# Fixing every engine's order by the source in a four-layer graph network, with row work spread in small steps

## The chip, the cores and the metric

The kernel runs on one core of a Trainium2 chip. The metric is the device time of one execution in microseconds (us). The core has a matrix engine (PE, TensorE), a vector engine (DVE), an activation engine (ACT, ScalarE), a general engine (POOL, GpSimd) and SP, whose queue issues the large transfers here. Each takes its instructions in the order of its own queue; semaphores let one wait for another.

## The reference

`x` has 4096 rows of 64 numbers, `adj` is a 4096 x 4096 matrix of zeros and ones. Four layers follow one another, each as `x = layernorm(x + layer(x, adj))`:

```python
# layer 0
deg = clip(sum(adj, axis=1) + 1, 1)
h = (adj @ x + x) / deg
z = relu(concat([x, h]) @ W + b)
out = z / max(norm(z), 1e-12)
# layers 1 and 3 (hyperbolic attention; logmap between every pair of rows)
x_t = logmap0(x)
adj_att = sigmoid(left[:, None] + right[None, :] + b_att) * adj    # left, right = x_t @ w_att halves
out = proj(expmap(x, einsum('ij,ijd->id', adj_att, logmap(x[:, None], x[None, :]))))
# layer 2
mask = adj != 0; rank = cumsum(mask, axis=1); deg = rank[:, -1:]
k = minimum(deg, 100); pos = rank - (deg - k)
out = (mask * where(pos > 0, 0.5 ** (k - pos), 0)) @ (x @ weight) + bias
```

## The kernel before

The rows are in 4 groups of 1024 (`GROUPS`, taken from 3 down to 0), the neighbours in 32 blocks of 128 (`BLOCKS`, from 31 down). Every layer reads the whole of `adj` again, as 64 loads of 1 MB (`load`, tile `edges`, five buffers, issued by SP at L614); one load holds two blocks for one group.

*Layer 0.* For each load PE multiplies both blocks with split values of x (L1087, four matmuls a block). `check` (L692) lets DVE look at every second load whether all its entries are zeros and ones. After 16 loads of a group ACT copies the sums out (`top`, L1107), PE multiplies them with the weights, and DVE divides by the degree (L1118). Then `end_0`, `norm_rows` and `prepare` follow for the group: they are the *row work*, dozens of dependent DVE operations on 128x8 numbers, some on 128x512 values, with copies on ACT (`ys`, `yd`, `hi_lo` and so on), transposes on PE (L775) and small products.

*Layers 1 and 3* (`attention`, `attend`). A *unit* is one block against one group of 1024 rows. PE forms the pair products `zp` in PSUM with six matmuls (L861, L864, L867), ACT makes `sig` (sigmoid, L869) and `sq` (square of zp, L873), DVE makes `t = max(zp, 0) * sig` (L875) and `t = (sq + const) * t` (L876), and PE adds `xe.T @ t` to the sums `acc` with two f32 matmuls (L878, four in the profile's count). `zp`, `sig` and `sq` have two buffers, `t` three. After 32 units ACT copies the sums, and `move` does the group's row work: 80 or so small operations, a Square and a tanh on ACT, two products on POOL (L912, L988), the last addition at L992. In layer 1 `linear` follows: transposes (L1001), a copy (`x_t`, L1004), products (L1008), halves by ACT (L1016) and DVE (L1017). `spread_left` (L837, L842) makes the left column of the next group for ACT.

*Layer 2* has two passes of two groups each. For 64 units a pass, PE forms the ranks `z` (L1209), ACT the weights `w` (exp, L1217), PE the sums (L1220). `end_2`, `norm_rows` and `prepare` are the row work behind it.

*The order.* Row work is written as generators in a list `waiting`, first in first out. `tick(rate)` runs the next steps of the first one between two units: three per load in layer 0, two, then one per unit in layer 1, four, then one in layer 3, one in layer 2. That is the order in the source only: the framework's scheduler reorders the instructions of each engine's queue as it thinks best before the kernel is built, and the pools of layer 1, 2 and 3 open and close between stages. A step's operations may all depend on each other. At the end a fallback under `If(fit < P)` is there; it was not taken.

Of the kernel before, what the change touches and what calls it, by code (L numbers as in the profile page):

```python
# [10 lines left out]
F32 = mybir.dt.float32  # L11
F16 = mybir.dt.float16
# [7 lines left out]
P = 128  # L20
N = 4096
D = 64
# [36 lines left out]
def gnn_stack_kernel(  # L59
# [511 lines left out]
    def stream(fits):  # L571

        with ExitStack() as st:

# [5 lines left out]
            loads = pool("f_loads", 5)  # L580
# [8 lines left out]
            waiting = []  # L589

            def tick(n):
                while n and waiting:
                    if next(waiting[0][1], False) is False:
                        waiting.pop(0)
                    else:
                        n -= 1

            def later(tag, *steps):
                def all_steps():
                    for part in steps:  # L600
                        yield from (part or ())

                waiting.append((tag, all_steps()))

            def need(tag):
                while any(t == tag for t, _ in waiting):
                    tick(1)
# [10 lines left out]
            def grp(name, bufs=None):  # L618
                kw = {"bufs": bufs} if bufs else {}
                return row.tile([P, WB, D], F32, name=name, **kw)  # L620

            def nums(name, n=WB):
                return row.tile([P, n], F32, name=name)
# [4 lines left out]
            def rsqrt(a, name):  # L628

                n = a.shape[1]  # L630
                half = row.tile([P, n], I32, name="rs_half")
                V.tensor_scalar(half, a.bitcast(I32), 1, None, ALU.logical_shift_right)
                r, t = nums(name, n), nums("rs_t", n)
                V.tensor_scalar(
                    r.bitcast(I32), half, -1.0, float(0x5F3759DF), ALU.mult, ALU.add
                )
                for _ in range(3):
                    V.tensor_mul(t, r, r)
                    V.scalar_tensor_tensor(t, t, -0.5, a, ALU.mult, ALU.mult)
                    V.scalar_tensor_tensor(r, t, 1.5, r, ALU.add, ALU.mult)  # L640
                return r
# [20 lines left out]
            ys = keep.tile([P, WB, 3 * D + 10], F16, name="ys")  # L662
            yd = keep.tile([P, WB, D + 10], F16, name="yd")
            es, ed = ys[:, :, 3 * D :], yd[:, :, D:]
            rest = (ROOT - 2.0) * UNIT
            for k in range(3):
                part = float(np.float16(rest))
                nc.gpsimd.memset(es[:, :, k], part)
                rest -= part
            nc.gpsimd.memset(ed[:, :, 0:3], 1.0)  # L670
            nc.gpsimd.memset(es[:, :, 3:5], 1.0)
            nc.gpsimd.memset(ed[:, :, 5:7], 1.0)

            def att_columns(w_att, name):


                w = row.tile([P, 2], F32, name="att_w")
# [18 lines left out]
            def curved(c, name):  # L696

                c2, sc = num(keep, name + "_c2", 1), num(keep, name + "_sc", 1)
                rsc, of_y = num(keep, name + "_rsc", 1), num(keep, name + "_of_y", 1)
                V.tensor_scalar(c2, c, -2.0, None, ALU.mult)  # L700
                V.tensor_copy(rsc, rsqrt(c, "rsc"))
                V.tensor_mul(sc, rsc, c)
                V.tensor_scalar(of_y, rsc, -((2.0 * UNIT) ** -0.5), None, ALU.mult)
                V.tensor_scalar(sc, sc, -((2.0 * UNIT) ** 0.5), None, ALU.mult)
                return c, c2, sc, rsc, of_y

            def norm_rows(x, s, v, x2_to):

                m, v2, sq = nums("n_m"), nums("n_v2"), grp("sq")
                V.tensor_reduce(m, v, AX.X, ALU.add)  # L710
                V.tensor_scalar(m, m, 1.0 / D, None, ALU.mult)
                yield 1
                V.tensor_sub(v, v, over(m))
                nc.scalar.activation(sq, v, AF.Square)
                yield 1
                yield 1
                V.tensor_reduce(v2, sq, AX.X, ALU.add)
                yield 1
                V.tensor_scalar(m, v2, 1.0 / D, 1e-5, ALU.mult, ALU.add)
                r = rsqrt(m, "n_r")  # L720
                yield 1
                V.tensor_mul(x[:, blocks(s), :], v, over(r))
                V.tensor_mul(x2_to, r, r)
                V.tensor_mul(x2_to, x2_to, v2)
                yield 1

            def prepare(s, x, att, b_att, curve, least, good):

                c, c2, sc, rsc, of_y = curve
                at, cols = blocks(s), slice(s * WW, (s + 1) * WW)  # L730
                xg, bg, rbg = x[:, at, :], b[:, at], rb[:, at]
                V.tensor_scalar(cx2[:, at], x2[:, at], c, None, ALU.mult)
                V.tensor_scalar(bg, cx2[:, at], -1.0, 1.0, ALU.mult, ALU.add)
                V.reciprocal(rbg, bg)

                V.tensor_scalar(rbg, rbg, -0.13, 0.0, ALU.max, ALU.min)

                m, y = nums("m"), grp("z0")
                V.tensor_scalar(m, rbg, sc, None, ALU.mult)
                V.tensor_mul(y, xg, over(m))  # L740
                nc.scalar.copy(ys[:, :, :D], y)
                yield 1
                nc.scalar.copy(ys[:, :, 2 * D : 3 * D], y)
                nc.scalar.copy(yd[:, :, :D], y)
                hl = row.tile([P, WB, 2], F16, name="hl")
                V.tensor_scalar(hl[:, :, 0], rbg, UNIT, None, ALU.mult)
                V.scalar_tensor_tensor(hl[:, :, 1], rbg, UNIT, hl[:, :, 0], ALU.mult, ALU.subtract)
                nc.gpsimd.tensor_copy(es[:, :, 5:7], hl)
                nc.gpsimd.tensor_copy(es[:, :, 7:9], hl)
                nc.gpsimd.tensor_copy(es[:, :, 9], hl[:, :, 0])  # L750
                nc.gpsimd.tensor_copy(ed[:, :, 3:5], hl)
                for k, of in ((7, 0), (8, 0), (9, 1)):
                    nc.gpsimd.tensor_scalar(
                        ed[:, :, k], hl[:, :, of], -2.0 / UNIT, None, ALU.mult
                    )
                V.tensor_sub(ys[:, :, D : 2 * D], y, ys[:, :, :D])
                yield 1

                g, w = nums("g"), grp("w_att")
                V.tensor_scalar(g, cx2[:, at], 1.0, 1.0 / D, ALU.add, ALU.mult)  # L760
                V.tensor_scalar(m, rbg, CUBE / UNIT, None, ALU.mult)
                V.tensor_add(w, xg, over(g))
                yield 1
                V.tensor_mul(xe[:, at, :], w, over(m))
                yield 1
                for into, rows_of in (
                    (hi_lo, ys[:, :, : 2 * D]),
                    (lo_hi, ys[:, :, D : 3 * D]),
                    (src, ys[:, :, 2 * D :]),
                    (dst, yd),  # L770
                ):
                    n = rows_of.shape[2]
                    t = aux.tile([P, WW], F16, name="aux")
                    for k in range(WB):
                        nc.tensor.transpose(  # L775
                            t[:n, k * P : (k + 1) * P], rows_of[:, k, :], ident16
                        )
                    yield 1
                    nc.scalar.copy(into[:, cols], t[:n])
                    yield 1  # L780


                q, q1, rt, t = nums("q"), nums("q1"), nums("rt"), nums("tt")
                V.tensor_scalar(q, x2[:, at], least, c, ALU.max, ALU.mult)
                V.tensor_scalar(q1, q, SMALL, None, ALU.max)
                rt = rsqrt(q1, "rt")
                yield 1
                V.tensor_mul(t, q1, rt)
                V.tensor_scalar(t, t, TOP, None, ALU.min)
                V.tensor_scalar(q1, q1, QTOP, None, ALU.min)  # L790
                nc.scalar.activation(t, t, AF.Ln, bias=1.0)
                nc.scalar.activation(q1, q1, AF.Ln, bias=1.0, scale=-1.0)
                yield 1
                f = nums("f")
                V.tensor_scalar(q, q, SMALL, SHIFT, ALU.min, ALU.add)
                V.scalar_tensor_tensor(q, q, 0.2, q, ALU.mult, ALU.mult)
                yield 1
                V.scalar_tensor_tensor(f, q1, -0.5, t, ALU.mult, ALU.add)
                V.tensor_mul(f, f, rt)
                V.scalar_tensor_tensor(f, f, SERIES0, q, ALU.add, ALU.add)  # L800
                V.tensor_scalar(m, bg, of_y, None, ALU.mult)
# [528 lines left out]
```

## Time and profile before

| what | value |
|---|---|
| median of 3 runs | 1247.65 us (1246.52 to 1258.46) |
| the profiled execution | 1248.49 us, its span 1246.8 us |
| mean granted clock of PE | 0.95 |
| busy: PE, DVE, ACT, POOL | 85%, 79%, 65%, 4% of the span |
| L875 and L876, mean of one | 1219 and 1220 ns, 256 each |
| L869 and L873, mean of one | 1143 and 1114 ns, 256 each |
| L692 (`check`) | 2288 ns, 64 |
| loads of `edges` | 256 of 1 MB |

The stages, as the first big instruction of each shows them in the timeline:

| stage | from, us | to, us |
|---|---|---|
| layer 0 (first load issued to first L875) | 5.0 | 223.5 |
| layer 1, starts of the groups | 223.5, 311.9, 412.1, 513.0 | 597.4 (last L875) |
| layer 2 (L1217) | 619.5 | 854.8 |
| layer 3, starts of the groups | 860.7, 960.4, 1042.4, 1129.3 | 1215.0 (last L875) |
| last group's row work, store, fallback's test | 1215.0 | 1246.8 |

A line such as "PE aux L775 <- DVE ys L756: 25.8, 5, 7.6" means: PE's instructions of L775 waited 25.8 us in total for DVE's instruction of L756, 5 times, the longest 7.6 us. In a timeline each row has its start, its length, the engine, the line and the operation, and in brackets the idle time of the engine before it and what ended that. The digits of the busy rows are tenths of 40 equal slices.

### The profile page before, as it was taken

How to read it: one execution, taken by the hardware profiler on the slowest of the kernel's cores; microseconds unless marked ns; L12 is line 12 of the kernel's file. 1: busy time of each engine (PE TensorE's matmuls, PEld its weight loads, DVE VectorE, ACT ScalarE, POOL GpSimd, SP SyncE). 2: the span in 40 equal slices, each digit the busy share in tenths (PEclk: the TensorE clock that was granted, in tenths of full speed). 3: DMA queues.
4: the chain of work that ended last, by engine and by line, in shares of the span. 5: the costliest groups of instructions: out<-in, count | busy, mean ns of one | idle time of the engine just before them, and what ended most of it. 6: DMA issues, size and time to landing. Idle time of an engine off the chain costs nothing.

```text
span 1246.8 us, 13844 instructions
## 1 busy us (share of the span) xinstructions
PE 1064.1 (85%) x4818; PEld 393.4 (32%) x4907; DVE 981.3 (79%) x2081; ACT 811.4 (65%) x833; POOL 49.6 (4%) x85
## 2 busy tenths in 40 slices
PE   5879788899998899798598898898889999899990
PEld 2345445232222322322232223332333333222220
DVE  5486876999997799599663347535999999999996
ACT  0021213889886787587365668767889888788870
POOL 0010101000000000000100000000000000001001
PEclk9989899899999799699699999999999999999996
DMA  7989898555554366155177887688345555565510
GB/s 280 400 338 335 313 357 324 186 175 203 202 203 169 109 201 229 68 203 186 51 268 271 295 313 265 241 295 299 134 152 201 203 202 203 182 204 204 203 34 20
DMA packets 40144, 271.83 MB, mean 218 GB/s; under 512 B 6016, under 2 KB 6272, under 8 KB 7296
## 3 DMA queue, kind: packets, MB, share of 16 engines
q1 hardware_dynamic: 37440, 269.50, 61.0%
q10 hardware_dynamic: 2624, 1.35, 0.4%
q8 instruction: 40, 0.66, 0.2%
q14 instruction: 40, 0.33, 0.1%
HBM read 269.78 MB, written 1.05 MB: 217 GB/s over the span
## 4 chain that ended last, share of the span: by engine, by line
DVE 40%; PE 40%; ACT 12%; DMA 4%; issue 3%; POOL 1%; another core or an unknown queue 0%; ACTq 0%; POOLq 0%; SPq 0%; DVEq 0%
DVE t L875 14%; DVE t L876 13%; PE acc L878 7%; PE z L1209 6%; PE acc L1220 6%; ACT w L1217 5%; PE zp L861 4%; PE zp L864 4%; PE zp L867 4%; PE acc L1087 4%; ACT sq L873 3%; DVE junk L692 3%; DMA edges<-in_adj_dram 2%; PE aux L1008 2%; PE aux L775 1%
## 5 line engine op out<-in xcount | busy, mean ns | idle before, releaser
L873 ACT ACTIVATE sq<-zp,turn 128x1024 f32<-128x1024 f32 x256 | 285.1, 1114 | 84.1 <-PE zp L867 52.9
L875 DVE SCALAR_TENSOR_TENSOR t<-zp,sig 128x1024 f32<-128x1024 f32 x256 | 311.3, 1219 | 15.3 <-ACT sq L873 12.9
L876 DVE SCALAR_TENSOR_TENSOR t<-sq,t 128x1024 f32<-128x1024 f32 x256 | 311.0, 1220 | 0.8
L869 ACT ACTIVATE sig<-left_b,right 128x1024 f32<-128x1024 f32 x256 | 292.1, 1143 | 19.9 <-DVE t L875 18.0
L878 PE MATMUL acc<-t,xe 128*64 128x512 f32 x1024 | 282.2, 624 | 16.6 <-DVE t L876 15.9
L692 DVE SCALAR_TENSOR_TENSOR junk<-edges 128x2048 bf16<-128x2048 f32 x64 | 146.4, 2288 | 94.2 <-DMA edges<-in_adj_dram 94.2
L861 PE MATMUL zp<-edges,two_i 128*128 128x512 bf16 x461 | 181.3, 393 | 37.8 <-DVE t L875 34.1
L864 PE MATMUL zp<-lo_hi,hi_lo 128*128 128x512 f16 x512 | 195.5, 382 | 3.7 <-issue 0.4
L867 PE MATMUL zp<-dst,src 74*128 74x512 f16 x512 | 196.7, 384 | 0.0
L1217 ACT ACTIVATE w<-z,at_edge 128x1024 bf16<-128x1024 f32 x128 | 136.1, 1113 | 76.3 <-PE z L1209 74.0
L861 PEld LDWEIGHTS <-two_i 128*128 128x128 bf16 x512 | 50.2, 98 | 178.9 <-issue 141.7
L1220 PE MATMUL acc<-w,halves 128*64 128x512 bf16 x512 | 80.9, 393 | 25.0 <-ACT w L1217 24.5
L1087 PE MATMUL acc<-edges,first 128*128 128x512 bf16 x240 | 79.0, 406 | 16.7 <-DMA edges<-in_adj_dram 16.3
L878 PEld LDWEIGHTS acc<-t,xe 128*64 128x64 f32 x1024 | 51.8, 136 | 124.5 <-DVE t L876 64.6
L1209 PE MATMUL z<-edges,enter 128*128 128x512 bf16 x245 | 85.4, 393 | 2.2 <-DVE k L909 1.6
L1087 PE MATMUL acc<-edges,third 128*65 128x512 bf16 x256 | 83.2, 407 | 0.8 <-issue 0.2
L867 PEld LDWEIGHTS <-src 74*128 74x128 f16 x512 | 49.4, 96 | 101.0 <-issue 42.2
L864 PEld LDWEIGHTS <-hi_lo 128*128 128x128 f16 x512 | 50.1, 98 | 86.0 <-issue 50.3
L1209 PE MATMUL z<-edges,pass_by 128*128 128x512 bf16 x237 | 75.0, 394 | 1.7 <-issue 1.5
L1220 PEld LDWEIGHTS <-halves 128*64 128x64 f16 x512 | 24.1, 108 | 75.6 <-issue 74.6
L1107 ACT COPY top<-acc 128x512 f32<-128x512 f32 x8 | 4.7, 588 | 63.7 <-PE acc L1087 63.7
L1209 PEld LDWEIGHTS <-enter 128*128 128x128 bf16 x256 | 24.2, 97 | 52.3 <-issue 28.9
(255 smaller groups left out, 784.4 us busy)
## 6 DMA issues: line engine op xcount, KB each, us to landing
edges<-in_adj_dram SPq DMA_DIRECT2D x256, 1024.0 KB, 5.0
x<-in_x_dram SPq DMA_DIRECT2D x4, 256.0 KB, 3.9
out_dram<-x ACTq DMA_DIRECT2D x4, 256.0 KB, 2.5
att_sb<-in_L_gnn_w_att_dram ACTq DMA_DIRECT2D x1, 64.0 KB, 7.3
att_sb<-in_L_gnn_att_w_dram ACTq DMA_DIRECT2D x1, 64.0 KB, 6.1
w_sb<-in_L_gnn_W_dram ACTq DMA_DIRECT2D x1, 32.0 KB, 3.7
b_sb<-in_L_gnn_b_dram ACTq DMA_DIRECT2D x1, 32.0 KB, 4.1
b_sb<-in_L_gnn_bias_dram ACTq DMA_DIRECT2D x1, 32.0 KB, 5.2
```

The source lines that it names most:

```text
L692: V.scalar_tensor_tensor(junk, a, 0.0, a, ALU.not_equal, ALU.not_equal, accum_out=odd[:, n : n + 1])
L861: nc.tensor.matmul(half, two_i, edge[:, at : at + W], start=True, stop=False)
L864: nc.tensor.matmul(half, hi_lo[:, of], lo_hi[:, to], start=False, stop=False)
L867: nc.tensor.matmul(half, src[:, of], dst[:, to], start=False, stop=True)
L869: nc.scalar.activation(sig, left_b, AF.Sigmoid, bias=right[:, j : j + 1])
L873: nc.scalar.activation(sq, zp, AF.Square, bias=turn, scale=-1.0 / UNIT)
L875: V.scalar_tensor_tensor(t, zp, 0.0, sig, ALU.max, ALU.mult)
L876: V.scalar_tensor_tensor(t, sq, HIGH**2, t, ALU.add, ALU.mult)
L878: nc.tensor.matmul(acc[h * D : (h + 1) * D, :], xe[:, j, :], t[:, h * W : (h + 1) * W], start=j == BLOCKS[0], stop=j == BLOCKS[-1],)
L1087: nc.tensor.matmul(accs[h][:m], lhs[:, j, :], edge[:, at : at + W], start=j == BLOCKS[0], stop=j == BLOCKS[-1],)
L1209: nc.tensor.matmul(z[:, h : h + W], lhs, rhs[:, h : h + W], start=j == BLOCKS[0], stop=True, skip_group_check=True,)
L1217: nc.scalar.activation(w, z, AF.Exp, bias=at_edge, scale=-LN2)
```

## The change

- A scheduling mode (`manual_schedule`) keeps the order of the source in every engine's queue.
- In attention a unit's sums are issued one unit later: the queue of PE holds the pairs of unit j and then the sums of unit j-2 or j-1 (`lag`, `flush(1)`); in layer 2 one behind (`flush(0)`). At a group's end the copy of its sums stands behind the last sums in the same list.
- Row work is cut into levels: nearly every dependent operation is a step of its own, and independent ones share a step. `tick()` stands between L875 and L876 (new L1274 and L1276), `tick(2)` after; six steps per load in layer 0, two per unit in layer 2. Row tiles are doubled by the group's parity (`own_rows`, `yss`, `yds`).
- Layer 0's boundary section (weights' product and degree) becomes the first steps of the next group's row work; `spread_left` is put at the front of the row work from the tenth load of the group before on.
- `prepare` advances its vectors and its norm's logarithm in turns (`both`); so do the two groups' chains after each pass of layer 2.
- Arithmetic is shortened: one shift less in `rsqrt`, constants fused, `move`'s ACT copy (L906) gone (DVE reads PSUM).
- Buffers: six for loads, two for `t`; pools of attention and layer 2 are opened once; ACT's small transfers at the start stand in a row.

Counted in the queues: PE 7717 instructions as before, DVE 1976 for 2020, ACT 826 for 837, POOL 93 for 87. Core of the diff:

```diff
+            st.enter_context(tc.manual_schedule())
...
-            loads = pool("f_loads", 5)
+            loads = pool("f_loads", 6)
...
+            def both(*steps):
+                steps = list(steps)
+                while steps:
+                    steps = [part for part in steps if next(part, waiting) is not waiting]
+                    yield
...
+            def flush(keep):
+                while len(lag) > keep:
+                    for add in lag.pop(0):
+                        add()
...
-                half = row.tile([P, n], I32, name="rs_half")
-                V.tensor_scalar(half, a.bitcast(I32), 1, None, ALU.logical_shift_right)
...
                 V.tensor_scalar(
-                    r.bitcast(I32), half, -1.0, float(0x5F3759DF), ALU.mult, ALU.add
+                    r.bitcast(I32), a.bitcast(I32), -0.5, float(0x5F3759DF), ALU.mult, ALU.add
                 )
+                yield
...
-                nc.scalar.copy(of.rearrange("p (h k) f -> p h k f", h=2), t)
-                yield 1
-                V.tensor_reduce(sum_1, of, AX.X, ALU.add)
...
+                V.tensor_reduce(sum_1.rearrange("p (h k) -> p h k", h=2), t, AX.X, ALU.add)
+                yield
+                V.tensor_scalar(k, sum_1, 1.0 / D, None, ALU.mult)
+                yield
+                for h in range(2):
+                    V.tensor_sub(
+                        halves_of[:, h], t[:, h],
+                        k[:, h * SB : (h + 1) * SB, None].to_broadcast([P, SB, D]),
+                    )
+                held.pop()
+                yield
+                nc.gpsimd.tensor_mul(w, xg, u)
+                nc.scalar.activation(sq, u, AF.Square)
...
+                        if g < 6 and next_left is None and n + 1 < NW and not held:
+                            need((layer, "dst", GROUPS[n + 1]))
+                            if not held:
+                                next_left, steps = spread_left(layer, GROUPS[n + 1])
+                                waiting.insert(0, steps)
...
+                            flush(1)
...
-                        t = sb.tile([P, WW], F32, name="t", bufs=3)
+                            t = sb.tile([P, WW], F32, name="t")
                             V.scalar_tensor_tensor(t, zp, 0.0, sig, ALU.max, ALU.mult)
+                            tick()
                             V.scalar_tensor_tensor(t, sq, HIGH**2, t, ALU.add, ALU.mult)
+                            tick(2)
...
-                        tick(3)
+                        tick(6)
...
+                            flush(0)
...
+                            lag.append([add])
+                            tick(2)
+                lag[-1].append(
+                    lambda two=two, accs=accs: later(
+                        both(*[end_2(s, sums_of(s, acc)) for s, acc in zip(two, accs)])
+                    )
+                )
```

## The prediction

> **What bounds the kernel now.** I read the busy digits and the chain of waits first, then the timeline of one undisturbed stretch, then the waits, then the boundary between two groups.
>
> ```profile
> PE   5879788899998899798598898898889999899990
> DVE  5486876999997799599663347535999999999996
> PEclk9989899899999799699699999999999999999996
> DVE 40%; PE 40%; ACT 12%; DMA 4%; issue 3%; POOL 1%; another core or an unknown queue 0%; ACTq 0%; POOLq 0%; SPq 0%; DVEq 0%
> ```
>
> Slices are 31.2 us. Layer 0 fills slices 1 to 7, attention 8 to 19 and 28 to 39, layer 2 those between. In attention DVE stands at 9 except at a few holes, where the clock row dips too. So attention is DVE's, layer 2 is PE's, layer 0 nobody's. A unit without row work:
>
> ```profile
> 303.56 1.23 DVE L876 SCALAR_TENSOR_TENSOR t<-sq,t 128x1024 f32<-128x1024 f32 x1
> 304.70 1.22 DVE L875 SCALAR_TENSOR_TENSOR t<-zp,sig 128x1024 f32<-128x1024 f32 x1
> 305.96 1.22 DVE L876 SCALAR_TENSOR_TENSOR t<-sq,t 128x1024 f32<-128x1024 f32 x1
> ```
>
> From L875 to the L876 that needs it is 1.26 us, from there to the next L875 1.14: 2.39 us a unit, 32 units 76.6 us a group. PE needs 2.37 us for the same unit (six pair matmuls 0.217 apart, two sums of 0.48, some 0.1 of change) and ACT 2.26 (1.143 + 1.114). No engine has room for one late hand-off.
>
> The starts of the groups (first L875 of each) are 88.4, 100.2 and 100.9 us apart in layer 1, 99.8, 81.9 and 86.9 in layer 3. Adding up the whole DVE queue of each group by durations of the timeline (a small operation 0.077 us if the next does not need its result, 0.20 if it does, as at 395.0; 0.60 for 512 columns) gives 84.8, 87.3, 85.5 and 95.0, 79.6, 83.3. What is over is waiting: 3.6, 12.9, 15.4 in layer 1, 4.8, 2.3, 3.6 in layer 3. The 13 and 15 are these boundaries:
>
> ```profile
> 395.10 1.08 PE L878 MATMUL acc<-t,xe 128*64 128x512 f32 x4
> 400.09 0.63 PE L1001 MATMUL aux<-ident,x 128*64 128x128 f32 x4 [3.91 <-DVE x L992]
> 401.39 1.96 PE L1008 MATMUL aux<-w_sb,x_t 64*128 64x64 f32 x8 [0.67 <-ACT x_t L1004]
> ...
> 406.96 2.12 PE L837 MATMUL aux<-ident,left 128*128 128x128 f32 x8
> 408.87 1.06 PE L891 MATMUL aux<-ident,sums 128*128 128x128 f32 x4
> 413.39 0.58 PE L861 MATMUL zp<-edges,two_i 128*128 128x512 bf16 x1 [3.46 <-DVE t L875]
> ```
>
> The end of a row chain, the linear products and the spread of the next group's left column stand one behind the other between two groups, in front of the next pairs. The same happens at 497 and 598.
>
> ```profile
> PE aux L775 <- DVE ys L756: 25.8, 5, 7.6
> DVE deg L1118 <- PE aux L1115: 22.9, 8, 6.2
> DVE junk L692 <- DMA edges<-in_adj_dram: 94.2, 28, 9.4
> ACT w L1217 <- PE z L1209: 74.0, 55, 2.8
> PE acc L878 <- DVE t L876: 15.9, 24, 3.7
> ```
>
> Columns: total us, times, longest. The first two are layer 0's (PE idle some 7 us at 79, 131 and 182; one serial section per boundary), the third layer 0's late loads, the fourth layer 2's PE.
>
> **The change, part by part.** All differences are against the profiled execution: 1248.49 us, span 1246.8, 0.84 above the median shown. Numbers of lines in the changed kernel are marked "new".
>
> *Layer 0.* A group's loads start 51.4 us apart on the mean (50.9, 103.5, 154.5, 205.1). Sums: PE 42 at full clock, DVE 39.4 (38.9 before), transfers 40 to 42 for 16 MB at the best slice's 400 GB/s. Removed: the serial section at the boundary and one of the two waits above, up to 9 us a group; at best 4 x 9 = -36, less the start that no order shortens, so -30. Added: with 96 steps in 16 loads of 6, PE stands in order behind the 0.58 us x_t copies (twice), the 1.02 us turned copies and `ys`, and DVE behind PE's answers; four to six such hops of 0.7 to 1.5 us, I take 7 us. One buffer more for loads helps only where transfers are late. I take -5 for the stage, since the new waits are those that I can count; +12 if each group keeps its 7 us idle and gets one more check behind it.
>
> *Row work in levels, 3 steps a unit.* The step between the two big DVE instructions is free: it stands where 0.118 us of dependence lay idle. Two that follow each other after the second cost 0.20 + 0.07, so a unit costs 2.66. With the 512-wide rows of a move (five of 0.60 and two halves of 0.345) the queue is 88.7, 87.2, 87.2, 87 in layer 1 and 97.2, 86.6, 86.6, 84.2 in layer 3. In layer 3 that is 2.2, 7.0, 3.3 and 3.0 above before, which had its steps one to a unit, nearly free. Sixty-odd operations gone (TENSOR_SCALAR 684 to 640 among those of 128x8, the copy L906 of 0.59 on ACT) are in these sums.
>
> *Order by the source.* Each hand-off now stands in its engine's queue whether its input is there or not. Per group: the copy of the sums, on ACT before the next sigmoid, waits for the last sum: 0.55, its transposes 0.3. `Square` (new L956) follows the DVE subtractions that come after L876's successor and stands ahead of the next sigmoid; the next first product waits for both: hop 0.1 + 0.62 + 1.14, so 1.9. The tanh 0.1, the spread 0.2 to 0.9. In layer 1 the transposes of x (new L1065) stand ahead of the next pairs and wait for an addition that DVE does some 4.9 us later: pairs late by 2.5, sums and products 0.5 to 0.9 later, 3.2 together. Behind them on PE stand the pairs, and for these ACT's square and DVE.
>
> Half a clock follows. At the boundary shown PE was idle 3.91 us, and matmuls of the same form then ran at twice the spacing from 400.8 to 417.8; an idle of 2.5 us at 1065.3 left the clock whole. An idle of 4.9 is on the far side: 6.8 us at half speed (the shortest such spell after one long idle), of which DVE sees about 2. Without the throttle the term is 0.
>
> The Trainium skill ("TensorE: Matmul & The Clock Gate", HAM oscillation) puts the gate at idle gaps above about 3.4 us; by that rule the 4.9 us costs the slow spell and the 2.5 us stalls cost none, as in my terms. The same page's ramp penalty, under 1% of a span, would make the whole term less than 12 us by an estimate from its figure. It speaks against a change that puts PE's waits in line; that two such waits can lie in one window no row here shows.
>
> Sum by stage, new minus old. Layer 1, group 1: queue 88.7 plus the preparation of the last group in line (three 0.62 copies, four 1.02 turned copies, two logarithms with two table loads of 1.28, partly beside DVE: 7) = 95.7 against 88.4: +7 (0 to +12). Groups 2 and 3: 87.2 + 6.7 + 2 = 96 against 100.2 and 100.9: -9 (-24 to +4; the low end has no stall at all). Group 4 and the change to layer 2: 106.5 before (513.0 to 619.5, of it 22 without a big product), 94 to 103 after, -6 (-18 to +4). Layer 3, group 1: two chains in turns put eight 1.02 copies, two times three of 0.62 and two Squares in ACT's queue, 14 us of which DVE hides the smaller part: 97.2 + 11 = 108 against 99.8: +9 (0 to +16). Groups 2 to 4: +13 of queue, +10 of stalls, less the 10.5 of waiting that was there: +13 (+2 to +24). The tail, two dependent copies and some steps shorter: -2.
>
> *Layer 2.* 64 units of 1.724 us are PE's, 110 a pass; ACT has 0.6 free a unit. Two chains in turns put two turned copies (2.04) behind one 1.11 exponential, against a lead of one unit: 0.7 to 1.4 late at four places, logarithms with tables 2.5 once a pass; sums one unit behind save PE part of its waits for L1217 (24.5 in all over 51). +4 (-8 to +14).
>
> *Two buffers for t instead of three, pools no longer opened anew, start-up DMAs in a row.* The sum of unit j-1 is done before product j+1 needs the buffer, with some 1.8 us to spare, so nothing; if a late sum took it, it is inside the stalls above. Pools: in the change to layer 2. DMAs: before the first loads are used.
>
> Sum: -5 + 7 - 9 - 6 + 9 + 13 + 4 - 2 = +11, so 1248.5 + 11 = 1259.5, say 1260.
>
> **The rivals.** *(a) The boundaries vanish and the stalls hide.* For it: 13 + 15 + 22 us of waiting at three places are really taken away, 30 more in layer 0, and zp's lead of 2.2 us over DVE could swallow a Square. Against it: each stall above is longer than the 0.3 us that ACT and PE regain in a unit. Stalls halved (49 us over eight groups to 25: -24) and layer 0 at -27 give 1260 - 24 - 22 = 1214. Break-even of attention lies at 49 us of stalls, 6 a group: my own sum, so the sign hangs on it.
>
> *(b) In-line waits throttle PE.* If PE idles more than once in a stage beyond 3.9 us (linear in layers 0 and 1, preparation in layers 1 and 3), half clock makes PE the bound: 4.7 us a unit against 2.66, 2 us each over three or four units at some five places: +35, 1295. The point from which it decides: a second idle of over 3.4 us before the first spell's end. For it: L775's waits. Against it: layer 3 has no linear step.
>
> *(c) Order doesn't matter.* The order listing shows other orders on all engines, so only an exact exchange would leave 1248.
>
> **How the numbers follow.** My forecast, that stalls are exchanged for stalls, gets 0.49, (a) 0.36, (b) 0.12, (c) 0.03. Within 1% (12.5 us, about what can be told from no change) lie 0.16 of the forecast, (c) and 0.02 of (a): 0.21. Slower: 0.31 of the forecast and (b), 0.43. Faster: 0.34 of (a) and 0.02 of the forecast, 0.36. The forecast's own range is 1240 to 1285 (stalls -20 or +25). The range of 8 in 10 takes in most of (a) and the nearer half of (b): 1203 to 1293.
>
> **What would show it.** Right: groups 2 and 3 of layer 1 at about 96 us, those of layer 3 at 90, ACT rows with idle "<-DVE u" at new L956, PE idle of some 5 us ahead of new L1065, layer 0 near 50 us a group, the two starts of layers 1 and 3 longer than before. Wrong by (a): layer 1 at 90 or less and layer 0 at 44 a group. Wrong by (b): clock digits of 5 to 8 inside groups.

## The result, and the profile after

The changed kernel takes 1291.68 us (median of 4, 1290.78 to 1296.18) against 1248.68 us for the kernel before beside it: 3.4% slower, ratio 1.0336 with a 95% interval of 1.0276 to 1.0396. The sign was forecast, the size was not: +11 us were worked out, +43 measured, 1.3 us inside the upper end of the range. The profiled execution took 1290.78 us, its span is 1289.0 us. The stages, in us, from the first big instruction of each:

| stage | before | after | difference | predicted |
|---|---|---|---|---|
| layer 0 to the first product of attention | 223.5 | 227.0 | +3.5 | -5 |
| layer 1, group 1 | 88.4 | 99.2 | +10.8 | +7 |
| layer 1, groups 2 and 3 | 201.0 | 203.5 | +2.5 | -9 |
| layer 1, group 4 and change to layer 2 | 106.5 | 110.4 | +3.9 | -6 |
| layer 2, two passes to layer 3's first product | 241.2 | 219.6 | -21.6 | +4 |
| layer 3, group 1 | 99.7 | 111.3 | +11.6 | +9 |
| layer 3, groups 2 to 4 | 254.5 | 289.5 | +35.0 | +13 |
| tail | 31.8 | 28.5 | -3.3 | -2 |

The page after, with the same rows as were shown of before:

```profile
PE   4779788779888888897799998987698888888882
DVE  2786775879898798798764484249698988988987
PEclk9999897989999898998899999998899988999996
PE 24%; DVE 18%; ACT 6%; issue 3%; ACTq 0%; POOL 0%; POOLq 0%; DVEq 0%
```

DVE's row is even now, but at 7 to 9 where it had been 9 with holes: the large holes became many small ones. (The chain is traced back over half of the span only, so its shares cannot be set beside those of before.) The waits, total us, times, longest:

```profile
DVE t L1274 <- ACT sq L1272: 106.0, 51, 17.2
PE z L1257 <- DVE t L1274: 80.3, 123, 3.4
PE aux L771 <- DVE ys L828: 23.3, 3, 9.3
DVE deg L1150 <- PE aux L1144: 13.4, 5, 3.9
DVE junk L722 <- DMA edges<-in_adj_dram: 63.2, 19, 11.6
ACT w L1379 <- PE z L1370: 54.6, 110, 1.7
PE acc L1283 <- DVE t L1276: 5.8, 10, 1.4
```

The first line is the story: DVE's first product (L1274, L875 before) waits 106 us for ACT's square, where the same wait was 12.9 us before. PE's wait for the sums' input fell from 15.9 to 5.8, as the lag was meant to do. Layer 0's wait for `ys` is nearly as it was, 23.3 for 25.8.

Where the first product waits shows in one unit of layer 3's second group, first ACT, then DVE:

```profile
981.91 0.63 ACT L956 ACTIVATE sq<-u 128x512 f32<-128x512 f32 x1 [4.17 <-DVE u L949]
982.44 1.13 ACT L1268 ACTIVATE sig<-left_b,right 128x1024 f32<-128x1024 f32 x1
983.48 1.09 ACT L1272 ACTIVATE sq<-z,turn 128x1024 f32<-128x1024 f32 x1
```

```profile
979.98 1.22 DVE L1276 SCALAR_TENSOR_TENSOR t<-sq,t 128x1024 f32<-128x1024 f32 x1
981.13 0.75 DVE L949 TENSOR_TENSOR u<-aux,b 128x256 f32<-128x256 f32 x2
984.61 1.22 DVE L1274 SCALAR_TENSOR_TENSOR t<-z,sig 128x1024 f32<-128x1024 f32 x1 [2.74 <-ACT sq L1272]
```

ACT stands idle 4.17 us because the row work's Square is next in its queue and its input is not there. DVE makes the input at 981.1 to 981.9, then waits while ACT does Square, sigmoid and the unit's own square, 2.7 us in all. The first product reads `sig` and the pair products (`z` here, `zp` before) only, and yet in both kernels not one of the 256 begins before the unit's square has ended (0.031 us after it at the soonest). The program asks for this: sigmoid and square add to one semaphore of ACT (at 983.58 and 984.59 here), and in the changed kernel as built each of the 256 first products waits for the count that its unit's square reaches.

In layer 3's group 3 most units with small row work take 2.67 to 2.68 us from first product to first product. In front of a first product DVE stands idle for 2.45 us at the copy of the sums (a unit of 4.93 us), 2.74 at the Square (5.88), 0.80 at the tanh (3.67), 2.61 at the end (5.69) and 0.58 behind it: 9.2 us. The 2.61 at the end is due to a transfer; the rows are those of the same place in group 2:

```profile
1052.34 0.37 ACTq L1406 DMA_DIRECT2D out_dram<-x  x1
1052.76 1.15 ACT L1268 ACTIVATE sig<-left_b,right 128x1024 f32<-128x1024 f32 x1 [5.51 <-DVE x L1056]
1053.81 1.09 ACT L1272 ACTIVATE sq<-z,turn 128x1024 f32<-128x1024 f32 x1
```

The output's store is issued from ACT's queue and waits there for the last addition, with the next sigmoid behind it: ACT is idle for 5.51 us. In layer 1 the transposes of the linear step do the same on PE's queue:

```profile
509.22 1.03 PE L1065 MATMUL aux<-ident,x 128*64 128x128 f32 x4 [5.41 <-DVE x L1056]
510.05 0.63 PE L1257 MATMUL z<-edges,two_i 128*128 128x512 bf16 x1
```

### The profile page after: what moved, and what is told of

It is laid out like the page before. It is cut to its first block, busy times and chain, and to the rows that moved or that the text cites. A ratio compares the mean times of both kernels' runs of the same rounds, so it can differ in the third digit from the quotient of the medians.

```text
span 1289.0 us, 14020 instructions
## 1 busy us (share of the span) xinstructions
PE 1064.2 (83%) x4817; PEld 382.9 (30%) x4907; DVE 987.4 (77%) x2037; ACT 798.3 (62%) x819; POOL 49.1 (4%) x91
## 4 chain that ended last, share of the span: by engine, by line
PE 24%; DVE 18%; ACT 6%; issue 3%; ACTq 0%; POOL 0%; POOLq 0%; DVEq 0%
PE z L1370 9%; DVE t L1274 8%; DVE t L1276 5%; PE acc L1386 5%; PE acc L1283 3%; ACT sq L1272 2%; PE z L1257 2%; PE z L1260 2%; PE z L1263 2%; ACT w L1379 1%; ACT sig L1268 1%; PE aux L771 1%; ACT sums L625 0%; PE aux L912 0%; DVE q L667 0%
## 5 line engine op out<-in xcount | busy, mean ns | idle before, releaser
L1274 DVE SCALAR_TENSOR_TENSOR t<-z,sig 128x1024 f32<-128x1024 f32 x256 | 312.1, 1219 | 114.3 <-ACT sq L1272 106.0
L1272 ACT ACTIVATE sq<-z,turn 128x1024 f32<-128x1024 f32 x256 | 284.2, 1110 | 97.7 <-PE z L1263 66.5
L1276 DVE SCALAR_TENSOR_TENSOR t<-sq,t 128x1024 f32<-128x1024 f32 x256 | 313.0, 1223 | 3.1
L1268 ACT ACTIVATE sig<-left_b,right 128x1024 f32<-128x1024 f32 x256 | 292.8, 1144 | 26.1 <-DVE x L1056 16.5
L1257 PE MATMUL z<-edges,two_i 128*128 128x512 bf16 x458 | 185.6, 405 | 80.9 <-DVE t L1274 80.3
L1260 PE MATMUL z<-lo_hi,hi_lo 128*128 128x512 f16 x512 | 201.5, 394 | 4.5 <-issue 1.1
L1263 PE MATMUL z<-dst,src 74*128 74x512 f16 x512 | 201.6, 394 | 0.0
L1379 ACT ACTIVATE w<-z,at_edge 128x1024 bf16<-128x1024 f32 x128 | 142.2, 1114 | 55.6 <-PE z L1370 54.6
L1195 PE MATMUL acc<-edges,first 128*128 128x512 bf16 x241 | 80.1, 409 | 25.2 <-DVE first L1118 16.5
L1370 PE MATMUL z<-edges,enter 128*128 128x512 bf16 x245 | 76.7, 391 | 4.2 <-DVE enter L1322 3.9
L771 PE MATMUL aux<-ident,ys 128*128 128x128 f16 (+1 forms) x192 | 17.2, 254 | 36.8 <-DVE ys L828 23.3
L1195 PEld LDWEIGHTS <-first 128*128 128x128 bf16 x256 | 24.5, 101 | 54.1 <-DVE first L1118 16.5
L1195 PEld LDWEIGHTS <-third 128*65 128x65 bf16 x256 | 29.4, 115 | 35.3 <-issue 6.3
```

What stands on the lines that cost most here:

```text
L1195: nc.tensor.matmul(accs[h][:m], lhs[:, j, :], edge[:, at : at + W], start=j == BLOCKS[0], stop=j == BLOCKS[-1],)
L1257: nc.tensor.matmul(half, two_i, edge[:, at : at + W], start=True, stop=False)
L1260: nc.tensor.matmul(half, hi_lo[:, of], lo_hi[:, to], start=False, stop=False)
L1263: nc.tensor.matmul(half, src[:, of], dst[:, to], start=False, stop=True)
L1268: nc.scalar.activation(sig, left_b, AF.Sigmoid, bias=right[:, j : j + 1])
L1272: nc.scalar.activation(sq, zp, AF.Square, bias=turn, scale=-1.0 / UNIT)
```

## The experiments

My theory: ACT's and PE's row work stands in the queue where the source has it, ahead of the next unit, and each such hand-off makes DVE wait for the rest of ACT's unit as well. Rivals: the small levels take all lead from the engines, so a stall moved shows up elsewhere; the buffers; the clock.

**One hand-off moved (e2_square).**

```diff
                 nc.gpsimd.tensor_mul(w, xg, u)
+                yield
                 nc.scalar.activation(sq, u, AF.Square)
                 yield
                 yield
+                yield
+                yield
```

> The changed kernel with one edit: the Square of the row work in attention is issued one step later, so that ACT's queue has it behind the next unit's square instead of ahead of the next unit's sigmoid; three empty steps in all, so that what follows keeps its place. Theory (in-order hand-offs on ACT): the unit with the Square falls from 5.87 us to about 3.1 in every group, 2.7 us x 8 groups = 21 us, 1291 to 1270. Rival (the levels leave no engine any lead, whatever is moved shows up at the next hand-off): the unit gets shorter and the following ones longer, total within 5 us of 1291.

1279.43 us, span 1275.3. The unit fell from 5.87 to 3.05 us in all six groups that have it. The sum in the expectation counted 8 groups; `move` runs inside attention in 6 (it is the work of the group before), and 6 x 2.7 = 16 stands against 13.7 of span. By groups 2.7, 1.5 and 2.0 us went in layer 1 and 4.3, 2.7 and 0.9 in layer 3: 0.9 came back at the linear step of layer 1's group 3 and some 2 in two units near the end of layer 3's last group. So the rival explains a small part at most.

**All of ACT's hand-offs of the move (e6_act_late).** A helper `act_slot` passes empty steps until the step between the two big products has come.

```diff
+            def act_slot(n=0):
+                for _ in range(n):
+                    yield
+                while slot[0] != 1:
+                    yield
...
+                            slot[0] = 2
                             tick(2)
+                            slot[0] = 1
...
+                yield from act_slot()
+                sums = sums_of(s, acc)
...
+                yield from act_slot()
                 nc.scalar.activation(sq, u, AF.Square)
...
+                yield from act_slot(1)
                 nc.scalar.activation(th, un, AF.Tanh, scale=lam)
...
+                yield from act_slot()
                 nc.scalar.dma_start(out[:, blocks(s), :], x[:, blocks(s), :])
```

> The changed kernel with all of ACT's row work in attention's move and store (copy of the sums, Square, tanh, the output's transfer) issued only in the step between the two big DVE products, so that in ACT's queue each stands behind a square and its input is there. The linear step of layer 1 and the preparation are left as they are. Theory (in-order hand-offs): saves 2.3 (sums), 2.7 (Square), 1.4 (tanh) in 8 groups and 2.7 (store) in 3 groups, up to 59 us: about 1240. Rival (levels leave no lead): less than a third of it, 1272 to 1291.

1243.31 us, 48 less than the changed kernel. Layer 3's groups 2 to 4 are 87.6, 87.5 and 85.2 us: within 1.0 of the sums of DVE's queue in the prediction (86.6, 86.6, 84.2). So levels cost what they were put at, and all else in these groups was the hand-offs and what followed from them. The first product's wait:

```profile
DVE t L1288 <- ACT sq L1286: 48.9, 22, 18.7
```

The clock went along with it. One stretch of 96 us in layer 3, the second group of the changed kernel, and in e6_act_late 69 us of the second and 27 of the third (columns: us; busy us of PE, PEld, DVE, ACT, POOL; clock; DMA share; GB/s), changed kernel first:

```profile
971.00:1067.00 96.00, 82.21 (x319) 25.36 (x324) 84.71 (x147) 69.69 (x68) 2.83 (x2) 0.95 0.48 171
```

```profile
971.00:1067.00 96.00, 87.95 (x357) 27.81 (x364) 95.03 (x166) 78.90 (x76) 3.25 (x2) 1.00 0.58 198
```

**The linear step spread too (e7_late).**

```diff
-                yield from linear(s, x, w2_sb, finish)
+                for _ in range(6):
+                    yield
+                yield from both(late(s, x, 0), late(s, x, 1))
```

`late` is one half of `linear` with its copies at `act_slot(1)` and its products three steps behind the copy.

> The changed kernel with ACT's row work of attention behind the squares (as in e6_act_late) and, new, layer 1's linear step spread: its transposes two units behind the addition that they read, each copy in the step between the two big products, the products a unit later, both halves in turns. Order still by the source. Theory (hand-offs in source order): the unit of 7.2 to 7.6 us in layer 1's groups 2 to 4 and the one of 3.8 behind it fall to 2.7, some 5.8 us in 3 groups: 1243 to about 1226. Rival (PE's queue has no place for them, the stall moves): 1238 or more.

1232.05 us, 11 less. Layer 1's groups 2 to 4 lost 5.9, 5.9 and 4.8, as expected; layer 2's first pass gave 7.4 of the 16.6 back. The spread chain runs into it: its last products and halves stand at 600 to 604 us, inside the pass's first unit of 7.66 us, and the next three units take 2.8, 4.6 and 3.4. The total lies between the two forecasts; the theory holds for the stall.

**Order by the source alone undone (e3_scheduler).**

```diff
-            st.enter_context(tc.manual_schedule())
```

> The changed kernel without the scheduling mode: the framework reorders every queue as it did before the change, all else (levels, lag, buffers, shorter arithmetic, turns) is the changed kernel's. Theory (in-order hand-offs): the scheduler puts ACT's row work where its input is ready, layer 3's groups 2 to 4 come back from 96 to 85 us or so, layer 1's boundaries may come back in part: 1225 to 1255. Rival (the levels themselves cost, DVE's queue of 87 us a group plus lost lead): 1275 or more.

1195.4 us, far under the expected 1225: ratio to the kernel before 0.9557 (0.9498 to 0.9615). The whole rest of the change gains 4.4%, and the source order takes that and 3.4% more, 96 us between the two. It is the fastest version found. Layer 1's groups are 87.8, 85.6, 89.9, 89.3 us (the last with the change to layer 2), layer 3's 100.6, 85.5, 85.5, 83.6: the boundaries of layer 1 are gone whole, not in part as expected. Behind layer 0, DVE's row in the page has no hole left but layer 2 and the change into layer 3:

```profile
DVE  5585956899999899899874386319999999999996
```

and the first product's wait is a quarter of the changed kernel's, 22.7 us of it the one at the change into layer 3:

```profile
DVE t L1273 <- ACT sq L1271: 28.5, 11, 22.7
```

**Which part takes the boundary of layer 1 away.** Four runs. First the rate of the row work in the kernel before:

```diff
-                1, x1, x_2, curve1, (2, 1, 1, 1), lambda s, x: linear(s, x, w2_sb, supports)
+                1, x1, x_2, curve1, (2, 2, 2, 2), lambda s, x: linear(s, x, w2_sb, supports)
...
-            attention(3, x_3, x_new, curve3, (4, 1, 1, 1), store)
+            attention(3, x_3, x_new, curve3, (4, 2, 2, 2), store)
```

> The kernel before with one edit: two steps of row work a unit instead of one in groups 2 to 4 of both attention layers. Theory (the boundaries stood there because the row work of the group before was not done by the group's end): layer 1's groups 2 and 3 fall from 100 to 86 or 90 us and its change to layer 2 by some 10, 1252 to about 1215. Rival (the scheduler would collect the steps at the boundary anyhow, since steps are large and dependent): 1240 or more.

1243.9 us, ratio 0.9946 (0.9912 to 0.998); the units that span the boundaries are still 19.1 and 19.5 us long (19.7 and 20.8 before), and most of the little that was gained is in layer 3's last group (81.7 us for 85.7). This theory (row work unfinished in the source) fell. Next, all of the change with the scheduler, but the left column at the boundary:

```diff
-                        if g < 6 and next_left is None and n + 1 < NW and not held:
+                        if g < 0 and next_left is None and n + 1 < NW and not held:
```

> The kernel of e3_scheduler (all of the change but the source order) without making the next group's left column ahead: it is made at the boundary, as before the change. Theory (the row work in levels, three steps a unit, is done before the group ends, and so nothing stands in the boundary but the column): 1197 to 1207. Rival (the column made ahead is what took the boundary away): the 13 to 17 us come back at three boundaries, 1230 or more.

1215.65 us; boundary units of 15.4 and 16.1 us are back and groups 2 and 3 are 97.3 and 96.9. The total lies between the two forecasts; for the boundary itself the rival holds (group 4 is 3.8 us shorter instead and layer 2's first pass 6.2 longer, for which no run here gives the reason). PE's queue there reads:

```profile
400.62 0.63 PE L1064 MATMUL aux<-ident,x 128*64 128x128 f32 x4 [1.31 <-DVE x L1055]
401.92 1.10 PE L1075 MATMUL aux<-w_sb,x_t 64*128 64x64 f32 x8 [0.67 <-ACT x_t L1069]
...
405.57 2.12 PE L911 MATMUL aux<-ident,left 128*128 128x128 f32 x8
```

The column's tiles come from the same two `aux` buffers as those of the linear step, and after them in the source. Last the column alone in the kernel before, at two places:

```diff
+                    if g == 3 and ahead is not None:
+                        left_b_next = spread_left(ahead)
...
-                        if n + 1 < NW:
-                            left_b = spread_left(GROUPS[n + 1])
```

> The kernel before with one part of the change: the next group's left column is made during the group (in front of the unit pair of its 13th load) instead of at the boundary. Theory (the boundary of layer 1 is the column's place behind the linear step in PE's queue, its two auxiliary PSUM buffers taken in turn): layer 1's groups 2 and 3 fall from 100 to 87 to 90 us, 1252 to about 1228; the change to layer 2 has no column and stays. Rival (the column ahead needs the small levels with it): 1245 or more.

1250.69 us, ratio 1.0017 (0.9997 to 1.0037): nothing. At the 13th load the linear step had begun in the source, and in PE's queue the column still stood behind it, at 408.1 us behind linear products from 402.5 to 408.

```diff
-                    if g == 3 and ahead is not None:
+                    if ahead is not None and g == (12 if ahead < GROUPS[1] else 3):
```

> The kernel before with the next group's left column made in the group's fifth load for groups 2 and 3, so that in the source, and in PE's queue as built, it comes ahead of the linear step of the row work (in e15_before_ahead it came behind, and stayed in the boundary). Theory (the column behind the linear step is the boundary): layer 1's groups 2 and 3 fall from 100 to about 87 us, the change to layer 2 stays, about 1224. Rival (the small levels are needed for it too): 1240 or more.

1233.88 us, ratio 0.9861 (0.9794 to 0.9928). The column now runs at 317.6 us and the linear step at 415.4. Groups 2 and 3 go from 100.2 and 100.8 to 82.0 and 91.5 us, the units that span the boundaries are 1.2 and 3.7 us long, and 9.4 come back in group 4 and the change to layer 2 (115.9 us for 106.5). So the column's place ahead of the linear step takes the two boundaries, without levels. With the whole change and the scheduler (e3_scheduler) nothing comes back in group 4 (89.3 us); which part of the change keeps it was not isolated.

**Layer 2.**

```diff
                             lag.append([add])
+                            flush(0)
                             tick(2)
```

> The changed kernel with layer 2's sums issued right behind their exponential in the source instead of behind the next ranks. Theory (the lag of one unit took PE's wait for the exponential away): layer 2's unit goes back from 1.56 us to the 1.775 that it had before, 128 x 0.215 = 27 us longer, 1318. Rival (the gain in layer 2 came from the sixth load buffer and the two chains in turns): within 6 us of 1291.

1472.11 us, a miss: the unit is 2.89 us, not 1.775. In strict source order PE waits in line for the exponential of the very unit, 1.26 us each time. Then the kernel of e3_scheduler without the lag, by one line behind each `lag.append([add])`, in attention too, and the same at a group's end:

```diff
                             lag.append([add])
+                            flush(0)
```

> The kernel of e3_scheduler with every unit's sums issued in the source right behind their unit, as before the change. Theory (with a scheduler the lag in the source is only a hint, the scheduler has it anyway): within 6 us of 1195 and layer 2 within 4 us a pass of 110 and 118. Rival (the lag is what gains in layer 2): layer 2's passes go back to 115 and 126, 1208 or more.

1210.22 us: the passes go from 109.8 and 118.2 to 120.4 and 125.3, attention stays within 2 us a group, and layer 2's unit goes from 1.56 back to 1.775 us in the median, that of the kernel before. The rival held: the lag in the source is what shortens layer 2's unit. The exponentials with it (changed kernel) and without (before):

```profile
714.59 1.11 ACT L1379 ACTIVATE w<-z,at_edge 128x1024 bf16<-128x1024 f32 x1 [0.45 <-PE z L1370]
716.15 1.11 ACT L1379 ACTIVATE w<-z,at_edge 128x1024 bf16<-128x1024 f32 x1 [0.45 <-PE z L1370]
```

```profile
700.48 2.12 ACT L1217 ACTIVATE w<-z,at_edge 128x1024 bf16<-128x1024 f32 x2 [1.43 <-PE z L1209]
704.03 1.11 ACT L1217 ACTIVATE w<-z,at_edge 128x1024 bf16<-128x1024 f32 x1 [1.43 <-PE z L1209]
```

Before, two exponentials ran together and then waited 1.43 us: 3.55 us a pair, 1.775 a unit. With the lag each follows after 1.56.

**Source order for layer 2 only (e10_mixed).**

```diff
+            fixed = ExitStack()
+            fixed.enter_context(tc.manual_schedule())
             for n in range(0, NW, 2):
...
+            fixed.close()
             x_4 = xs.tile([P, NB, D], F32, name="x")
```

> The kernel of e3_scheduler with the source order in layer 2 alone, where the changed kernel was the faster one (103.3 and 116.3 us a pass against 109.8 and 118.2 with the scheduler). Theory: 8 us less, 1187. Rival (the seams between the two modes cost more than that): 1195 or more.

1206.23 us, 11 slower than e3_scheduler: the passes took 115.2 and 121.0 us for 109.8 and 118.2, and the group ahead of them 94.0 for 89.3. The rival held. What in the seam costs this was not settled.

**The buffers (e5_t3).**

```diff
-            loads = pool("f_loads", 6)
+            loads = pool("f_loads", 5)
...
-                            t = sb.tile([P, WW], F32, name="t")
+                            t = sb.tile([P, WW], F32, name="t", bufs=3)
```

> The changed kernel, order by the source, with the buffers of before: three for t, five for the loads. Theory (neither sets an end: DVE's first product waits for the sums 7.8 us in all, 4 times): within 6 us of 1291. Rival (two buffers for t hold DVE back after each stall): 1280 or less.

1297.91 us, 6 more. By the profiled executions, 8.6 apart in span, all of it lies in layer 0 (231.9 for 227.0) and layer 2 (223.0 for 219.6), which have no `t`: there the sixth load buffer gains, 3.4 of layer 2's 21.6 us. Each group of layer 1 and each of layer 3 stays within 0.5 us: two buffers for `t` cost nothing in this order.

## Why the prediction was right or wrong

The direction was right, and for the reason given: in attention, stalls at hand-offs in the source's order. That the time fell into the range is in part luck. The stages other than layer 2 cost 57 us more than their terms in all, and layer 2 came out 25.6 us better than its own; with its +4 the time would have been some 1317 us, outside the range.

- *DVE's queue sums* were right: 2.66 us for a unit with row work against 2.67, and 86.6, 86.6, 84.2 a group against 87.6, 87.5, 85.2 once the hand-offs are away (e6_act_late).
- *The hand-offs* had the right mechanism and place and the wrong size: some 3.3 us a group in layer 3 against 9.2 of DVE's idle time. Four terms were short. Square 1.9 against 2.7, because the product waits for ACT's square of the unit too, 1.1 us more, which the term left out. The sums 0.85 against 2.45, with the same square in the wait. The tanh 0.1 against 0.8. The store 0 against 2.6: its issue on ACT's queue was not counted at all. Three groups times 5.9 are 18 of the 22 us missed there.
- *Layer 1.* The linear stall was put at 3.2 and 2 for the clock; DVE waited 4.9 us from 509.1 on, with an idle of 5.41 on PE (4.9 predicted) and pairs at double spacing. In the other two groups DVE waited 4.7 and 5.6; the spells at half speed there lasted 3.4, 6.8 and 6.8 us (6.8 predicted). The term held as a sum of 5.2; how it divides into stall and clock no run separates. The sums, Square and tanh were missed as in layer 3, and the later copies and halves (periods of 3.39, 2.89 and 4.25 us), put at 0.5 to 0.9, held DVE for 2.9 us a group.
- *Layer 2* failed as a step: "64 units of 1.724 us are PE's" took the unit as PE's own work. No row shows 1.724: before, a unit takes 1.775 us, with waits of PE for the exponential in it, and after it 1.56, with PE's matmuls back to back, so PE needs 1.56 at most. 128 x 0.215 = 27.5 us were there to gain; 21.6 were gained, and e11_sched_no_lag shows, under the scheduler, that the unit's 0.215 comes with the lag.
- *Layer 0*: the start was not costed. In order, DVE's second instruction waits 13.3 us for a small transfer, and the first product with `edges` comes at 16.5 instead of 13.8 us. PE's idle for `ys`, of which one wait a group was to go, stayed: 6.4, 7.7 and 9.3 us at the boundaries for 7.6, 7.0 and 6.8.
- *Rivals.* The time lies near rival (b)'s 1295, but hardly by its mechanism: half-speed spells followed stalls (clock 0.95 in layer 3, 1.00 with the hand-offs moved), and in layer 3's groups 2 to 4 DVE waited some 3 of its 32 us of idle time for matmuls in them (1.15 us the longest, at 1060 us for late sums). The clock's 0.938 over the span is 80 us of full clock lost, for 62 before: 18 more, where the prediction had an estimate of less than 12; how much of it reached the time no run separates. Rival (a) named the right gain for the boundaries, three large waits, and e3_scheduler has it; it needs another order than the source's.

## What to carry to other kernels

In a fixed order an engine that worked ahead lost its lead here at instructions whose input came from an engine behind it (2.3 to 2.7 us of DVE's time in layer 3 at the copy of the sums, the Square and the store). So list for every queue, DMA issues among them, what stands behind each cross-engine instruction, and place it after the next unit's work. The framework's scheduler found a better order by itself here: give it the better source (lag, the next group's input made ahead of the long chain) before taking it away. A unit's time read as an engine's own should be checked for the waits inside it.

## What the runs showed of the hardware

After an idle of PE, matmuls ran at half speed for a spell, but not always from the first one on. Two idles of 3.40 us in the changed kernel, at 982.5 and at 541.1:

```profile
985.88 0.39 PE L1257 MATMUL z<-edges,two_i 128*128 128x512 bf16 x1 [3.40 <-DVE t L1274]
...
987.59 1.98 PE L1283 MATMUL acc<-t,xe 128*64 128x512 f32 x4
```

```profile
544.51 0.59 PE L1257 MATMUL z<-edges,two_i 128*128 128x512 bf16 x1 [3.40 <-DVE t L1274]
```

After the first the matmuls ran at full spacing for about 1 us, and then the four sums of a unit took 1.98 us for 1.08 else; after the second they were slow from the start. In the clock records of the changed kernel's trace all 26 spells begin on one grid of 3.413 us and all but the last, at the program's end, last one, two or three of its steps; the spells here begin at 986.9 and 543.2. The two idles lie differently on that grid: the first begins 4.4 us ahead of its spell, the second 2.1.

The length of an idle alone did not decide either. At the same place, the store in layer 3's group 2, an idle of 3.22 us was followed by half speed in the changed kernel and 3.23 us was not in e2_square:

```profile
1056.21 0.59 PE L1257 MATMUL z<-edges,two_i 128*128 128x512 bf16 x1 [3.22 <-DVE t L1274]
```

```profile
1050.44 0.39 PE L1260 MATMUL z<-edges,two_i 128*128 128x512 bf16 x1 [3.23 <-DVE t L1277]
```

The Trainium skill ("TensorE: Matmul & The Clock Gate", HAM oscillation) has the gate close at gaps above about 3.4 us. The three gaps of 5.3 to 5.4 us ahead of the linear step, each with a slow spell, agree; the 3.22 us here and one of 2.79 us at 926.8, both with a spell, lie below that bound, and one of 3.50 us at 43.8 in e2_square, without a spell, above it. Here the measurement stands.

A spell is not a cost by itself: the one at 986.9 ended before DVE needed the next pairs, while in the one from 1055.2 to 1062.0 DVE waited 1.15 us for the sums. Why the program makes the first product wait for the square of its unit, which it does not read, no run here shows.
